# Layer 3 of a four-layer convolution kernel: two samples at a time, transfers over all partitions, a ring of 8 KB chunks

## The chip, the cores and the metric

The kernel runs on one core of a Trainium2 chip. The metric is the device time of one execution in microseconds; lower is better. A core has five engines that take their own instructions in order and meet through semaphores: TensorE (PE, the matmuls), VectorE (DVE), ScalarE (ACT), GpSimd (POOL) and SyncE (SP, which here only issues transfers). The 16 DMA engines move data between the chip's memory (HBM) and the on-chip buffer of 128 partitions (SBUF). Matmuls write to PSUM, and ScalarE or VectorE reads it from there.

## What is computed

The input is `x` with 16 samples, 16 channels and 256 x 256 pixels, in 32-bit floats. Four layers follow each other, each of the form "group norm, a convolution, add to x". The first is a circular 3 x 3 convolution written with Fourier transforms, the second a 5 x 5 convolution of diagonal kernels, the third a spectral layer with poles and residues. Only the fourth, layer 3, is changed:

```python
n = 2.0 ** (ACTBIT - 1) - 1.0                                  # 127
scale_input = jnp.max(jnp.abs(x_cl)) / 2.0 ** (ACTBIT - 1)     # over all samples
x_q = jnp.round(jnp.clip(x_cl / scale_input, -n, n))
acc = lax.conv_general_dilated(x_q, w_hwio, window_strides=(1, 1), padding=((1, 1), (1, 1)), ...)
out = acc * (scale_input * scale_weight) + bias
...
x = x + _L3_conv_ref(_gn(x), ...)
```

So each sample is normalised, divided by one scale that holds for all samples, rounded to whole numbers, clipped to +-127, convolved with a 3 x 3 kernel over 16 channels, scaled, and added to the sample as it came in. Because the scale is a maximum over everything, layer 3 can start on no sample before layer 2 has ended on all; layer 2 writes its result to HBM (`x3d`), and layer 3 reads it back.

## The kernel before

Layers 0 and 1 run together sample by sample, then layer 2 in several stages, then layer 3. Instructions of an engine stand in one fixed order. A scheduler makes that order when the program is built, from the program's text and the dependences between tiles; it puts work of a coming sample among that of the current one. A tile comes from a pool with a number of buffers (`bufs`): one more tile than there are buffers waits until the oldest has been read for the last time, by engines and by transfers.

Layer 3 before, lines 1180 to 1253 (the last `with ExitStack()` of the function `layers`), takes one sample b after the other.

- A sample's 256 rows of 16 channels are laid out as 64 partitions (16 channels times 4 strips s of 64 rows), and a strip is cut into 4 groups g of R = 16 rows. Partitions 0 to 63 (half a = 0) hold groups 0 and 3, partitions 64 to 127 (half a = 1) groups 1 and 2. `of_half` (L1189) gives that view of a tensor in HBM for one half.
- A sample is one tile `xt4` of 32 KB per partition (2 groups x 16 rows x 256 pixels), in a pool of 3. It is loaded in 4 chunks of RC = 4 rows, each by two transfers of 64 partitions, 512 KB each, on the SP queue (L1226).
- For each chunk ScalarE normalises and scales to `u` (L1233, all 128 partitions at once; for the second chunk, the `moved` one, in four pieces of 64 partitions, L1230). VectorE rounds `u` in place by adding and subtracting a large number (L1234) and clips it to `q` in 16-bit floats (L1238 in four pieces, or L1236 at once). A piece moves a group from its partition half a to an operand half h, since the matmul reads 64 partitions of `q` (half h) and writes 64 partitions of PSUM (half a).
- `q` has two buffers, used in turn by even and odd samples, with zero columns at both sides set once, in layer 2's stage (L1132, L1133). GpSimd copies four halo rows to `qh` (L1241).
- The convolution is done in 8 tiles t of 2 rows (`conv`, L1192 to L1218): 9 taps times 4 combinations of (a, h), each a matmul of 64 x 64 weights over 512 columns, four of them side by side in the array. At the edge of a group a matmul is split into two of 256 columns, one reading the neighbouring group or `qh`. Tiles go 1, 2, ... 7, 0, because tile 0 needs the halo above. PSUM holds 4 tiles.
- ScalarE evicts each tile with scale and bias to `o` (L1245), VectorE adds it to the rows of `xt4` in place (L189, the helper `tt` called at L1248), and GpSimd issues the store of a finished chunk to `out`, again two transfers of 64 partitions (L1252). The first chunk goes out last, after tile 0.

What the changed lines depend on: the loads of a sample wait for all stores of the sample three before it, which had the same buffer. In ScalarE's order, the `u` of a coming sample stand among the evictions `o` of an earlier one.

The stage before (layer 2's last, L1002 to L1174) ends with statistics over all samples, the scale by which everything is divided, and the per-sample factors `a3` and `b3` (L1171), one column per sample, the same for both partition halves.

Of the kernel before, what the change touches and what calls it, by code (L numbers as in the profile page):

```python
# [49 lines left out]
F32 = mybir.dt.float32  # L50
BF16 = mybir.dt.bfloat16
AF = mybir.ActivationFunctionType
# [5 lines left out]
P = 128  # L58
C = 16
S = 4  # L60
R = 16
RC = 4
N = 256
# [101 lines left out]
def layers(ctx, tc, x, w0, w1, w3, sw, bias, ty, tx, p1a, p1b, p1c, p2a, p2b, p2c, resa, resb,  # L165
           const, rows, out):
    nc = tc.nc
    B = x.shape[0]
# [4 lines left out]
    dram = ctx.enter_context(tc.tile_pool(name="dram", bufs=1, space=DRAM))  # L173
    x2d = [dram.tile([C, N, N], F32, tag=f"x2d{b}", name=f"x2d{b}") for b in range(B)]
    x3d = [dram.tile([C, N, N], F32, tag=f"x3d{b}", name=f"x3d{b}") for b in range(B)]
# [822 lines left out]
    qs = [last_.tile([P, 2, R, 260], BF16, tag=f"q{k}", name=f"q{k}") for k in range(2)]  # L998


    with ExitStack() as es:
# [97 lines left out]
        with tc.manual_schedule(engines={mybir.EngineType.PE}):  # L1099
            before = None  # L1100
            exps = exponentials(0)
            for k in range(0, C, 2):
                for b in range(B):
# [25 lines left out]
                    if k == C // 2 and b == 0:  # L1129
                        wt = strip_weights(last_, w3, 9, BF16, "wt3", [(0, 0, 9, 0), (9, 0, 3, 1), (12, 6, 3, 2)])  # L1130
                        for q in qs:
                            Q.memset(q[:, :, :, 0:2], 0.0)  # L1132
                            Q.memset(q[:, :, :, 258:260], 0.0)  # L1133
# [46 lines left out]
    with ExitStack() as es:  # L1180
        xp = es.enter_context(tc.tile_pool(name="e_x", bufs=3))
        up = es.enter_context(tc.tile_pool(name="e_u", bufs=3))
        hp = es.enter_context(tc.tile_pool(name="e_h", bufs=2))
        rp = es.enter_context(tc.tile_pool(name="e_r", bufs=4))
        ps_c = es.enter_context(tc.tile_pool(name="e_ps", bufs=4, space=PSUM))
        half = [slice(0, 64), slice(64, P)]
        groups = ((0, 0), (1, 0), (1, 1), (0, 1))

        def of_half(d, a, rr):  # L1189
            g = slice(1, 3) if a else slice(0, 4, 3)  # L1190
            return d.rearrange("c (s g r) w -> (c s) g r w", g=4, r=R)[:, g, rr, :]

        def conv(q, qh, t):

            ps = ps_c.tile([P, 2, 2, N], F32, tag="ps_c", name="ps_c")
            work = [[], [], [], []]
            for dy in (0, -1, 1):
                for dx in (0, -1, 1):
                    near = 3 * (1 + dy) + 1 + dx
                    cols = slice(2 + dx, 2 + dx + N)  # L1200
                    r0 = 2 * t + dy
                    for n, (a, h) in enumerate(groups):
                        o = ps[half[a], h]
                        if 0 <= r0 and r0 + 2 <= R:
                            work[n].append((h, o, near, q[half[h], a, r0 : r0 + 2, cols]))
                            continue
                        for r in range(2):
                            if 0 <= r0 + r < R:
                                work[n].append((h, o[:, r], near, q[half[h], a, r0 + r, cols]))
                            elif n ^ 1 == n + dy:  # L1210
                                work[n].append((h, o[:, r], near, q[half[h], 1 - a, (r0 + r) % R, cols]))
                            else:
                                w = near if 0 <= n + dy < 4 else (9 if dy < 0 else 12) + 1 + dx
                                work[n].append((h, o[:, r], w, qh[half[h], int(dy > 0), cols]))
            for i in range(len(work[0])):
                for h, o, w, src in (work[n][i] for n in (0, 2, 1, 3)):
                    nc.tensor.matmul(o, lhsT=wt[half[h], w, :], rhs=src, start=i == 0, stop=i == len(work[0]) - 1)  # L1217
            return ps  # L1218

        for b in range(B):  # L1220
            xt = xp.tile([P, 2, R, N], F32, tag="xt4", name=f"xt4_{b}")
            q = qs[b % 2]
            for r in range(0, R, RC):
                rr = slice(r, r + RC)
                for a in range(2):
                    nc.sync.dma_start(xt[half[a], :, rr, :], of_half(x3d[b], a, rr))  # L1226
                u = up.tile([P, 2, RC, N], F32, tag="u", name="u")
                moved = r == RC
                for a, h in groups if moved else ():
                    nc.scalar.activation(u[half[h], a], xt[half[a], h, rr, :], AF.Identity,  # L1230
                                         bias=b3[half[a], b : b + 1], scale=a3[half[a], b : b + 1])
                if not moved:
                    nc.scalar.activation(u, xt[:, :, rr, :], AF.Identity, bias=b3[:, b : b + 1], scale=a3[:, b : b + 1])  # L1233
# [5 lines left out]
            qh = hp.tile([P, 2, 260], BF16, tag="qh", name="qh")  # L1239
            for h, k, a, r in ((0, 0, 0, R - 1), (0, 1, 1, 0), (1, 0, 1, R - 1), (1, 1, 0, 0)):  # L1240
                Q.tensor_copy(qh[half[h], k], q[half[1 - h], a, r])  # L1241
            for t in (*range(1, R // 2), 0):
# [3 lines left out]
                xr = xt[:, :, 2 * t : 2 * t + 2, :]  # L1246
                tt(V, xr, xr, o, ADD)
                if t == 0 or t > 1 and t % 2:  # L1248
                    r0 = 2 * t // RC * RC
                    rr = slice(r0, r0 + RC)  # L1250
                    for a in range(2):
                        Q.dma_start(of_half(out[b], a, rr), xt[half[a], :, rr, :])  # L1252
# [89 lines left out]
```

## Time and profile before

| what | value |
|---|---|
| time, median of 3 runs | 4583.26 us (4581.63 to 4588.8) |
| the profiled execution: time, span | 4588.1 us, 4586.3 us |
| layer 3 in it: last statistic read, first load issued, end | 4053.7, 4064.2, 4586.3 us |
| layer 3, from 4080 us: bytes moved, mean rate | 131.8 MB, 258 GB/s |
| layer 3, from 4080 us: share of the 16 DMA engines, loads and stores | 45.8% and 40.2% |
| a load of 512 KB (`xt<-x3d`), median from issue to landing | 12.5 us |
| a store of 512 KB (`out_dram<-xt`), median from issue to landing | 8.3 us |

The engines in 50-us stretches of layer 3 (start:end, length; then busy us and count of TensorE, its weight loads, VectorE, ScalarE, GpSimd; TensorE's granted clock as a share of full, DMA share, GB/s):

```profile
4170.00:4220.00 50.00, 30.70 (x491) 18.47 (x484) 39.47 (x41) 33.58 (x26) 13.26 (x17) 0.84 0.88 258
4270.00:4320.00 50.00, 31.87 (x492) 19.05 (x488) 38.80 (x42) 32.68 (x25) 13.48 (x17) 0.85 0.86 260
4370.00:4420.00 50.00, 32.79 (x568) 20.43 (x564) 39.66 (x43) 31.40 (x24) 14.00 (x18) 0.90 0.84 251
```

How to read the profile: it is one execution, recorded by the hardware. A line of the group table names a source line, an engine, an operation, what it writes and reads (output<-inputs), the shape and the count; then the busy time of all, the mean of one in ns, the idle time of the engine just ahead of them and what ended it. A wait is put down to the event that came last. The DMA share is the part of the 16 engines' time in which a packet was under way, whatever its rate.

### The profile page before, as it was taken

How to read it: one execution, taken by the hardware profiler on the slowest of the kernel's cores; microseconds unless marked ns; L12 is line 12 of the kernel's file. 1: busy time of each engine (PE TensorE's matmuls, PEld its weight loads, DVE VectorE, ACT ScalarE, POOL GpSimd, SP SyncE). 2: the span in 40 equal slices, each digit the busy share in tenths (PEclk: the TensorE clock that was granted, in tenths of full speed). 3: DMA queues.
4: the chain of work that ended last, by engine and by line, in shares of the span. 5: the costliest groups of instructions: out<-in, count | busy, mean ns of one | idle time of the engine just before them, and what ended most of it. 6: DMA issues, size and time to landing. Idle time of an engine off the chain costs nothing. (4 is left out here: it accounts for less than half of the span.)

```text
span 4586.3 us, 123297 instructions
## 1 busy us (share of the span) xinstructions
PE 4004.8 (87%) x50992; PEld 3081.6 (67%) x50992; DVE 3077.3 (67%) x5698; ACT 2708.7 (59%) x3619; POOL 2270.4 (50%) x3562
## 2 busy tenths in 40 slices
PE   5999999999849998999899999997999999955655
PEld 1555555555529998999777777776788888833333
DVE  4767666767578787877655555544666667677767
ACT  3776868686524443444488888885444444446565
POOL 2242323233336555555566666655777777742323
PEclk9999999999979999999999999998999999978888
DMA  6676767685434444445377777777888888769888
GB/s 145 157 186 151 190 147 192 144 197 145 100 100 155 145 156 144 151 146 163 96 159 168 167 171 165 167 166 207 220 220 218 221 225 237 216 193 271 245 261 249
DMA packets 433391, 820.58 MB, mean 179 GB/s; under 512 B 43648, under 2 KB 308864, under 8 KB 417408
## 3 DMA queue, kind: packets, MB, share of 16 engines
q1 hardware_dynamic: 366272, 577.53, 50.2%
q0 software_dynamic: 66560, 235.18, 17.1%
q8 instruction: 402, 6.59, 0.7%
q14 instruction: 157, 1.29, 0.1%
HBM read 408.85 MB, written 336.07 MB: 162 GB/s over the span
## 5 line engine op out<-in xcount | busy, mean ns | idle before, releaser
L381 PE MATMUL ps<-va,wt 128*64 128x512 f32 (+1 forms) x1632 | 668.7, 571 | 11.4 <-POOL va L353 9.3
L381 PE MATMUL ps<-vb,wt 128*64 128x512 f32 (+1 forms) x1632 | 667.1, 570 | 4.7 <-DMA vb<-va 4.7
L877 ACT COPY sk<-ps_s 64x516 f32<-64x516 f32 x1016 | 592.6, 583 | 115.8 <-PE ps_s L872 96.3
L770 ACT ACTIVATE y<-ps_y,bc 128x384 f32<-128x384 f32 x512 | 296.9, 581 | 426.4 <-PE ps_y L768 426.4
L872 PE MATMUL ps_s<-t,l 128*128 128x258 f32 x2048 | 521.4, 397 | 17.8 <-ACT sk L877 8.4
L189 DVE TENSOR_TENSOR ob<-ps_m,other 128x256 f32<-128x256 f32 x512 | 270.9, 607 | 357.3 <-ACT other L965 352.8
L402 ACT ACTIVATE v<-xt,nm 32x2048 f32<-32x2048 f32 x248 | 497.1, 2005 | 9.7 <-PE ps L416 3.5
L416 PE MATMUL ps<-v,w1s 128*64 128x259 f32 x4096 | 481.6, 394 | 11.0 <-DVE v L400 6.7
L1217 PE MATMUL ps_c<-q,wt 64*64 64x512 bf16 (+1 forms) x4800 | 305.6, 403 | 207.1 <-ACT o L1245 179.2
L872 PEld LDWEIGHTS ps_s<-t,l 128*128 128x128 f32 x2048 | 371.1, 191 | 92.2 <-ACT sk L877 8.4
L381 PEld LDWEIGHTS ps<-va,wt 128*64 128x64 f32 x1632 | 223.2, 137 | 305.1 <-issue 271.2
L416 PEld LDWEIGHTS ps<-v,w1s 128*64 128x64 f32 x4096 | 335.2, 141 | 134.7 <-issue 24.0
L1079 PE MATMUL ps_o<-exp,fs 128*128 128x128 f32 x2048 | 404.6, 280 | 19.1 <-ACT fs L1125 19.1
L1217 PEld LDWEIGHTS <-wt 64*64 64x64 bf16 x4992 | 185.7, 115 | 326.8 <-issue 264.2
L1078 PE MATMUL ps_o<-c_last,zt 128*128 128x128 f32 x2048 | 404.1, 280 | 0.2
L1078 PEld LDWEIGHTS ps_o<-c_last,zt 128*128 128x128 f32 x2048 | 329.0, 196 | 63.2 <-issue 62.4
L940 PEld LDWEIGHTS ps_m<-z,sk 128*32 128x32 f32 x16384 | 254.6, 110 | 132.8 <-issue 111.4
L940 PE MATMUL ps_m<-z,sk 128*32 128x64 f32 x16384 | 304.0, 222 | 42.5 <-issue 38.5
L189 POOL TENSOR_TENSOR acc<-acc,prod 128x256 f32<-128x256 f32 x240 | 228.7, 953 | 217.3 <-DVE prod L189 210.8
L189 POOL TENSOR_TENSOR w<-rq 128x512 f32<-128x512 f32 x256 | 320.7, 1280 | 26.4 <-ACT rq L1080 23.6
L1079 PEld LDWEIGHTS ps_o<-exp,fs 128*128 128x128 f32 x2048 | 319.1, 197 | 20.1 <-ACT fs L1125 20.1
L765 PE MATMUL ps_y<-c_y,qd 128*128 128x128 f32 x2048 | 316.8, 278 | 5.3 <-ACT y L770 5.3
(345 smaller groups left out, 8910.0 us busy)
## 6 DMA issues: line engine op xcount, KB each, us to landing
xt<-x2d SPq DMA_DIRECT2D x256, 512.0 KB, 4.4
z<-alphad SPq DMA_DIRECT2D x516, 129.0 KB, 4.9
xt<-in_x_dram SPq DMA_DIRECT2D x256, 256.0 KB, 7.3
x2d<-x2s POOLq DMA_DIRECT2D x256, 256.0 KB, 5.0
mixd<-ob SPq DMA_DIRECT2D x128, 512.0 KB, 5.9
ot<-mixd SPq DMA_DIRECT2D x256, 256.0 KB, 7.3
x3d<-xt POOLq DMA_DIRECT2D x128, 512.0 KB, 5.8
xt<-x3d SPq DMA_DIRECT2D x128, 512.0 KB, 12.5
```

Of the source, the lines that this page charges most:

```text
L189: eng.tensor_tensor(o, a, b, op)
L381: nc.tensor.matmul(ps[halves[h], lo:hi, :], lhsT=wt0[:, w, :], rhs=v[:, 2 * t + lo : 2 * t + hi, j : j + N], start=j == 0 and k == 0, stop ...
L402: nc.scalar.activation(to, o.xt[c][q_], AF.Identity, bias=o.g.nm[q_, 1:2])
L416: nc.tensor.matmul(ps[halves[h], k, 0:U], lhsT=o.w1[:, w : w + 64], rhs=v1[:, lo : lo + U], start=first_, stop=not first_)
L765: nc.tensor.matmul(to[:, :, a, :], lhsT=v[:, c, a, i % 2, :], start=a == 0, stop=a == 1, rhs=y1[:, a].rearrange("p (r f) -> p r f", r=2))
L770: nc.scalar.activation(y[:, c, :], ps[:, 0 : 3 * P], AF.Copy, scale=bc2[:, b, i // 2, 0:1])
L872: nc.tensor.matmul(ps[:, d, 0 : 2 * NX], lhsT=ls[h][:, k + d - k0], rhs=t2[:, h, k + d].rearrange("p x r -> p (x r)"), start=True, stop=True)
L877: copy(sks[2 * e8 + n][64 * h : 64 * h + 64, :, 2 * k : 2 * k + 4] .rearrange("p x (k r) -> p x k r", r=2), ps[64 * n : 64 * n + 64, :, 0 ...
L940: nc.tensor.matmul(to, lhsT=sk[:, x_], rhs=z[:, :, x_], start=True, stop=True)
L1078: nc.tensor.matmul(ps[:, a, c, :], lhsT=zts[d][:, a, c, :], rhs=last[:, c, :], start=True, stop=False)
L1079: nc.tensor.matmul(ps[:, a, c, :], lhsT=fs[:, d, a, :], rhs=ey[:, d, c, :], start=False, stop=True)
L1217: nc.tensor.matmul(o, lhsT=wt[half[h], w, :], rhs=src, start=i == 0, stop=i == len(work[0]) - 1)
```

## The change

Layer 3 takes two samples a = 0, 1 at a time, one in each partition half, and every transfer spans all 128 partitions.

- A group now has R = 32 rows, so a strip has two groups h = 0, 1. A partition half is a sample, an operand half h is a half strip: the matmul for (a, h) reads `q[half h]` with index a and writes PSUM half a.
- `x3d` of two samples is one HBM tensor, and `by_strip` gives a view of 128 partitions (sample, channel, strip). A chunk is 4 rows of both half strips of both samples: one transfer of 1 MB, 8 KB per partition.
- Chunks are tiles of their own: chunk 0 of each pair from the pool `e_f` with 2 buffers (it is stored last), chunks 1 to 7 from `e_x` with 10. A chunk is stored as soon as both of its tiles are added, chunk 0 after tile 0.
- Chunks 1, 3, 5, 7 are `moved` (four ScalarE pieces, one clip on VectorE), the others the reverse.
- The pair is convolved in 16 tiles, 1 to 15 and then 0. Rows beyond a half strip come from `qh`, now with both samples in one copy (four copies of 64 x 2 x 260).
- `u` has 2 buffers for 3, `o` 3 for 4. `q` is twice as large, belongs to this stage's pools, and its zero columns are set at the start of it. `a3` and `b3` are copied to `a3p` and `b3p` with a column per pair (four small copies).

The built order on the engines follows the scheduler as before; on SP the 64 loads of 1 MB stand in the order of their chunks, with chunk 0 of a pair behind its chunks 1 to 3 from the third pair on. On GpSimd the stores stand in the order of the tiles, with the halo copies of the next pair among them: two behind the store of chunk 1, two ahead of that of chunk 7.

```diff
--- before.py
+++ after.py
@@ -58,7 +58,7 @@
 P = 128
 C = 16
 S = 4
-R = 16
+R = 32
 RC = 4
 N = 256
 NX = 129
@@ -172,7 +172,8 @@
 
     dram = ctx.enter_context(tc.tile_pool(name="dram", bufs=1, space=DRAM))
     x2d = [dram.tile([C, N, N], F32, tag=f"x2d{b}", name=f"x2d{b}") for b in range(B)]
-    x3d = [dram.tile([C, N, N], F32, tag=f"x3d{b}", name=f"x3d{b}") for b in range(B)]
+    x3p = [dram.tile([2, C, N, N], F32, tag=f"x3d{k}", name=f"x3d{k}") for k in range(B // 2)]
+    x3d = [x3p[b // 2][b % 2] for b in range(B)]
     alphad = dram.tile([N, 2, 2, 8, B // BG, NX, BG], F32, tag="alphad", name="alphad")
     mixd = dram.tile([N // 2, 4, C, 2, 2, B, 32], F32, tag="mixd", name="mixd")
 
@@ -995,7 +996,6 @@
     mn3 = last_.tile([P, G2], F32, tag="mn3", name="mn3")
     a3 = last_.tile([P, B], F32, tag="a3", name="a3")
     b3 = last_.tile([P, B], F32, tag="b3", name="b3")
-    qs = [last_.tile([P, 2, R, 260], BF16, tag=f"q{k}", name=f"q{k}") for k in range(2)]
 
 
     with ExitStack() as es:
@@ -1128,9 +1128,6 @@
                     before = (b, k, zts, fs, exps[1], xt)
                     if k == C // 2 and b == 0:
                         wt = strip_weights(last_, w3, 9, BF16, "wt3", [(0, 0, 9, 0), (9, 0, 3, 1), (12, 6, 3, 2)])
-                        for q in qs:
-                            Q.memset(q[:, :, :, 0:2], 0.0)
-                            Q.memset(q[:, :, :, 258:260], 0.0)
                 exps = coming
             along_x(*before)
 
@@ -1178,22 +1175,28 @@
 
 
     with ExitStack() as es:
-        xp = es.enter_context(tc.tile_pool(name="e_x", bufs=3))
-        up = es.enter_context(tc.tile_pool(name="e_u", bufs=3))
+        xp = es.enter_context(tc.tile_pool(name="e_x", bufs=10))
+        fp = es.enter_context(tc.tile_pool(name="e_f", bufs=2))
+        up = es.enter_context(tc.tile_pool(name="e_u", bufs=2))
         hp = es.enter_context(tc.tile_pool(name="e_h", bufs=2))
-        rp = es.enter_context(tc.tile_pool(name="e_r", bufs=4))
+        rp = es.enter_context(tc.tile_pool(name="e_r", bufs=3))
         ps_c = es.enter_context(tc.tile_pool(name="e_ps", bufs=4, space=PSUM))
+        qp = es.enter_context(tc.tile_pool(name="e_q", bufs=1))
+        qs = [qp.tile([P, 2, R, 260], BF16, tag=f"q{k}", name=f"q{k}") for k in range(2)]
+        for q in qs:
+            Q.memset(q[:, :, :, 0:2], 0.0)
+            Q.memset(q[:, :, :, 258:260], 0.0)
         half = [slice(0, 64), slice(64, P)]
-        groups = ((0, 0), (1, 0), (1, 1), (0, 1))
-
-        def of_half(d, a, rr):
-            g = slice(1, 3) if a else slice(0, 4, 3)
-            return d.rearrange("c (s g r) w -> (c s) g r w", g=4, r=R)[:, g, rr, :]
+        groups = [(a, h) for h in range(2) for a in range(2)]
+        chunks = R // RC
+
+        def by_strip(d):
+            return d.rearrange("b c (s h r) w -> (b c s) h r w", s=S, h=2)
 
         def conv(q, qh, t):
 
             ps = ps_c.tile([P, 2, 2, N], F32, tag="ps_c", name="ps_c")
-            work = [[], [], [], []]
+            work = [[] for _ in groups]
             for dy in (0, -1, 1):
                 for dx in (0, -1, 1):
                     near = 3 * (1 + dy) + 1 + dx
@@ -1207,49 +1210,53 @@
                         for r in range(2):
                             if 0 <= r0 + r < R:
                                 work[n].append((h, o[:, r], near, q[half[h], a, r0 + r, cols]))
-                            elif n ^ 1 == n + dy:
-                                work[n].append((h, o[:, r], near, q[half[h], 1 - a, (r0 + r) % R, cols]))
                             else:
-                                w = near if 0 <= n + dy < 4 else (9 if dy < 0 else 12) + 1 + dx
-                                work[n].append((h, o[:, r], w, qh[half[h], int(dy > 0), cols]))
+                                w = near if h == (dy < 0) else (9 if dy < 0 else 12) + 1 + dx
+                                work[n].append((h, o[:, r], w, qh[half[h], a, int(dy > 0), cols]))
             for i in range(len(work[0])):
                 for h, o, w, src in (work[n][i] for n in (0, 2, 1, 3)):
                     nc.tensor.matmul(o, lhsT=wt[half[h], w, :], rhs=src, start=i == 0, stop=i == len(work[0]) - 1)
             return ps
 
-        for b in range(B):
-            xt = xp.tile([P, 2, R, N], F32, tag="xt4", name=f"xt4_{b}")
-            q = qs[b % 2]
-            for r in range(0, R, RC):
-                rr = slice(r, r + RC)
-                for a in range(2):
-                    nc.sync.dma_start(xt[half[a], :, rr, :], of_half(x3d[b], a, rr))
+        a3p, b3p = (hp.tile([P, B // 2], F32, tag=k, name=k, bufs=1) for k in ("a3p", "b3p"))
+        for a in range(2):
+            for to, src in ((a3p, a3), (b3p, b3)):
+                V.tensor_copy(to[half[a]], src[half[a]].rearrange("p (k a) -> p k a", a=2)[:, :, a])
+        for k in range(B // 2):
+            q = qs[k % 2]
+            xs = []
+            for j in range(chunks):
+                rr = slice(RC * j, RC * j + RC)
+                pool = xp if j else fp
+                xt = pool.tile([P, 2, RC, N], F32, tag="xt4", name=f"xt4_{k}_{j}")
+                xs.append(xt)
+                nc.sync.dma_start(xt, by_strip(x3p[k])[:, :, rr, :])
                 u = up.tile([P, 2, RC, N], F32, tag="u", name="u")
-                moved = r == RC
+
+                moved = j % 2
                 for a, h in groups if moved else ():
-                    nc.scalar.activation(u[half[h], a], xt[half[a], h, rr, :], AF.Identity,
-                                         bias=b3[half[a], b : b + 1], scale=a3[half[a], b : b + 1])
+                    nc.scalar.activation(u[half[h], a], xt[half[a], h], AF.Identity,
+                                         bias=b3p[half[a], k : k + 1], scale=a3p[half[a], k : k + 1])
                 if not moved:
-                    nc.scalar.activation(u, xt[:, :, rr, :], AF.Identity, bias=b3[:, b : b + 1], scale=a3[:, b : b + 1])
+                    nc.scalar.activation(u, xt, AF.Identity, bias=b3p[:, k : k + 1], scale=a3p[:, k : k + 1])
                 V.tensor_scalar(u, u, ROUND, ROUND, ADD, SUB)
                 if moved:
                     V.tensor_scalar(q[:, :, rr, 2 : 2 + N], u, 127.0, -127.0, ALU.min, ALU.max)
                 for a, h in () if moved else groups:
                     V.tensor_scalar(q[half[h], a, rr, 2 : 2 + N], u[half[a], h], 127.0, -127.0, ALU.min, ALU.max)
-            qh = hp.tile([P, 2, 260], BF16, tag="qh", name="qh")
-            for h, k, a, r in ((0, 0, 0, R - 1), (0, 1, 1, 0), (1, 0, 1, R - 1), (1, 1, 0, 0)):
-                Q.tensor_copy(qh[half[h], k], q[half[1 - h], a, r])
+            qh = hp.tile([P, 2, 2, 260], BF16, tag="qh", name="qh")
+            for n, r in ((1, 0), (0, R - 1)):
+                for h in range(2):
+                    Q.tensor_copy(qh[half[h], :, n], q[half[1 - h], :, r])
             for t in (*range(1, R // 2), 0):
                 ps = conv(q, qh, t)
                 o = rp.tile([P, 2, 2, N], F32, tag="o", name="o")
                 nc.scalar.activation(o, ps, AF.Identity, bias=bi, scale=so)
-                xr = xt[:, :, 2 * t : 2 * t + 2, :]
+                j, r = divmod(2 * t, RC)
+                xr = xs[j][:, :, r : r + 2, :]
                 tt(V, xr, xr, o, ADD)
-                if t == 0 or t > 1 and t % 2:
-                    r0 = 2 * t // RC * RC
-                    rr = slice(r0, r0 + RC)
-                    for a in range(2):
-                        Q.dma_start(of_half(out[b], a, rr), xt[half[a], :, rr, :])
+                if t == 0 or j and r == RC - 2:
+                    Q.dma_start(by_strip(out[2 * k : 2 * k + 2])[:, :, RC * j : RC * j + RC, :], xs[j])
 
 
 def laid_out(inputs):
```

## The prediction

> **What bounds the kernel now.** Only layer 3, the last 530 us, is changed, so I read that stretch alone: who waits, then one turn of its loop in time order, then the rate of the transfers, then what each instruction costs. The waits from 4080 us to the end (who waited for whom, us in total, times, longest), the DMA-issuing queue's own in the second fence:
>
> ```profile
> PE ps_c L1217 <- ACT o L1245: 179.2, 56, 12.1
> ACT u L1233 <- DMA xt<-x3d: 161.2, 31, 12.8
> ```
>
> ```profile
> SPq L1226 <- DMA out_dram<-xt: 337.7, 52, 21.6
> ```
>
> Read from the bottom: the loads wait for stores, ScalarE waits for loads, TensorE waits for ScalarE to empty PSUM. ScalarE takes its instructions in order, and a normalisation of a coming sample (`u`) stands in front of evictions (`o`) of the current one. One such stop, in the timeline of ScalarE (start, length; idle before in brackets):
>
> ```profile
> 4282.13 2.29 ACT L1245 ACTIVATE o<-ps_c,bi,so 128x1024 f32<-128x1024 f32 x2
> 4295.87 2.09 ACT L1233 ACTIVATE u<-xt,b,a 128x2048 f32<-128x2048 f32 x1 [11.44 <-DMA xt<-x3d]
> 4297.87 1.19 ACT L1245 ACTIVATE o<-ps_c,bi,so 128x1024 f32<-128x1024 f32 x1
> ```
>
> The next stop ends at 4328.90, so a sample takes 33.0 us and a pair 66.0. The period is a closed loop: the last eviction of a sample started at 4274.86, its addition ended at 4279.19, its last store landed at 4287.79, the load into that buffer was issued at 4287.93, its second half landed at 4295.76, `u` started at 4295.87. In the next turn this loop latency is 20.0 us (4308.87 to 4328.90), and ScalarE needs 13.0 us from that `u` to the next last eviction: 20.0 + 13.0 = 33.0. So the stage is bound neither by an engine nor by bytes, but by buffer reuse: store, landing, load, landing.
>
> The rates, from the windows (length, ScalarE busy and count, granted clock, DMA share, GB/s):
>
> ```profile
> 4068.00:4092.00 24.00, 14.68 (x10) 0.68 1.03 221
> 4292.00:4298.00 6.00, 2.13 (x2) 0.75 1.02 222
> 4336.00:4342.00 6.00, 5.96 (x5) 1.00 1.02 399
> 4564.00:4582.00 18.00, 4.69 (x4) 0.80 0.99 369
> ```
>
> All DMA engines are busy in each row, yet they move 221 where loads of 64 partitions run alone and about 400 where loads and stores, or stores of both halves, overlap. The busy share hides a factor of two.
>
> The costs, from 4080 us on (busy us, mean ns | idle before):
>
> ```profile
> L189 DVE TENSOR_TENSOR xt<-xt,o 128x1024 f32<-128x1024 f32 x128 | 158.4, 1250 | 31.9 <-ACT o L1245 30.5
> L1245 ACT ACTIVATE o<-ps_c,bi,so 128x1024 f32<-128x1024 f32 x128 | 148.9, 1196 | 10.7 <-DVE xt L189 5.3 <-PE ps_c L1217 4.4
> L1233 ACT ACTIVATE u<-xt,b,a 128x2048 f32<-128x2048 f32 x47 | 98.3, 2092 | 164.9 <-DMA xt<-x3d 161.2 <-DVE q L1238 1.9 <-DVE q L1236 1.5
> L1230 ACT ACTIVATE u<-xt,b,a 64x1024 f32<-64x1024 f32 x60 | 74.1, 1235 | 1.4 <-DMA xt<-x3d 0.5
> ```
>
> Last, one transfer of 512 KB with nothing beside it, a load (4064.20) and a store (4342.23), from issue to landing:
>
> ```profile
> DMA to landing us min/median/max: 5.2/5.2/5.2
> ```
>
> ```profile
> DMA to landing us min/median/max: 4.6/4.6/4.6
> ```
>
> **What the Trainium skill says.** SBUF — State Buffer, section "Door 1: The DMA port swizzle": partitions 0 to 63 reach only 8 of the 16 ports, about 218 GB/s, and all 128 reach 16. The 221 and the 400 above agree. DMA: Bandwidth & Descriptors, section "Rules for kernel authors": use one transfer of 128 partitions instead of two of halves. Same page, section "Anatomy of one DMA": some 2 us of a transfer do not depend on its bytes. Here 512 KB at 221 GB/s is 2.4 us, which leaves 2.8 of the load's 5.2 and 2.2 of the store's 4.6: fixed cost, a little above that.
>
> **The change part by part.** *Transfers.* 1 MB over 128 partitions at 410 GB/s takes 2.6 us. Not seen before in this shape: estimate 2.8 + 2.6 = 5.4 us for a load, 2.2 + 2.6 = 4.8 for a store. The bounds: 4.6 and 4.4 if the fixed part is the skill's 2 us, 7.6 and 7.0 if the full width moves only 221. Three full-width loads of 512 KB at 1294 us landed 1.5 and 1.4 us apart, which speaks for the fast end.
>
> *Engine work per pair.* Of its 8 chunks 4 are normalised in four half-width pieces (2 of 8 before). ScalarE: 4 x 2.09 + 16 x 1.235 + 16 x 1.196 = 47.3 us (41.7 for two samples before). VectorE: 8 roundings x 1.24, 4 clips x 1.24, 16 half clips x 0.709, 16 additions x 1.25 = 46.2 (49.4 before). TensorE: 192 matmuls fewer, 16 tiles of 2.15 us at full clock = 34. None reaches 66, so these edits cost nothing by themselves while reuse sets the pace. GpSimd copies twice as many halo elements per copy (1.13 us before): 1 to 2 us, counted in the chain below.
>
> *The ring.* Chunks 1 to 7 of a pair take 10 buffers in turn, chunk 0 takes 2 of its own. So chunk 4+i of a pair reuses the buffer of chunk 1+i of the pair before it, chunks 1 to 3 that of 5 to 7 two pairs back, and chunk 0 that of chunk 0 two pairs back. ScalarE's built order in a steady turn, with t for an eviction of pair k and u for a normalisation of pair k+1 (four pieces in odd chunks): t1 t2 u0 t3 u1 t4 u1 u2 t5 u3 t6 u3 u4 t7 t8 u5 t9 u5 t10 u6 t11 u7 t12 u7 t13 t14 t15 t0. Chunk j is stored after tile 2j+1, chunk 0 after t0, which is the last tile. Each store-to-load path gives a wait if its latency exceeds ScalarE's work between its two ends:
>
> - H: t0 of a pair to u0 two pairs later stands only t0, t1, t2 apart: 3.6 us.
> - B: t5 to u5: four evictions, u3, u4: 11.8 us.
> - D: t9 to u7: three evictions, one piece of u5, u6: 6.9 us.
> - The others (t3 to u4 16.8, t11 to u1 17.8, t13 to u2 16.6, t15 to u3 18.7) are longer than the latency below; t7 to u6 (9.7) overlaps B and D and gives less.
>
> H, B and D do not overlap, so the turn is 47.3 - 3.6 - 11.8 - 6.9 = 25.0 us plus the three latencies. One latency, alone: eviction 1.27, addition 1.23, to the store's issue 0.3, store 4.8, to the load's issue 0.14, load 5.4, start 0.08: 13.2 us. B adds 0.2 for the rounding ahead of its addition on VectorE: 13.4. D: 13.2. H is worse: VectorE stands behind u7's rounding and clip and four additions (7.5 us from u7's end, 3.6 us ahead of t0), so the store is issued at 4.3 and not 2.8; GpSimd has the store of chunk 7 right before it, and loads of chunks 2 and 3 share the engines (2.6 us each): store landed near 11.7, load near 17.2. Sum 43.8, turn 68.8 us against 66.0. What is queued behind each stopped `u` is the evictions, and TensorE behind them with at most 4 tiles ahead. The gain in rate is thus spent: before, there was one reuse loop in 33 us, now three in 69.
>
> *Start and end.* Both first chunk-0 buffers lie where the last buffers of the stage before are free near 4055 us, so `u0` has its data when the scales are ready (4065 us, four tiny copies included). Chunk 1 is issued at 4064.2 as before, landed at 4069.6. From there no reuse wait binds in the first turn: u1 to u7 26.0, pair 1's u 28.1, 15 evictions 17.9, so t0 of pair 0 starts at 4141.7. Moving `q` out of the older pool shifts layer 2's tiles and puts three small loads on the SP queue ahead of that stage's first data: 3 x 0.55 = 1.6 us (0 to 3). So 4143. Then 6 turns: 413, to 4556. The last pair has no normalisations: 15 tiles x 2.0 us (spacing of evictions at the end of before) plus 4 for the clock, which falls to 0.5 in stops, then 2.8 to the store, 5.5 landing, 2.5 to the end: 44. Sum 4600 us against the profiled span of 4586.3: +13.5. The profiled execution took 4588.1 with what lies around its span; the median of the runs is 4583.3. I set the difference on the median: 4597.
>
> **Rivals.**
> - The latencies come out shorter: fixed parts of 2 us, no queueing in H: 12, 12 and 14.5. Turn 63.5, six turns save 32 us: 4565, faster. It decides in ScalarE's stops at u0, u5, u7: below 41.5 us in sum the turn falls under 66.5, the break-even. For it: 400 GB/s is seen. Against it: VectorE's backlog at t0 and three stores in 5 us.
> - The ring's waits are covered and ScalarE and VectorE set the pace, some 50 us a turn: 4597 - 6 x 18.8 = 4484. Against it: H's 3.6 us of cover for two transfers.
> - The full width is no faster than half, 7.6 and 7.0 per transfer: latencies near 17.6, 17.6, 23, turn 83, 4597 + 86 = 4683. Against it: the windows near 400.
>
> **How the numbers follow.** Forecast 0.68 (4575 to 4625: +-3 us on the sum of latencies, +-8 on the ends), short latencies 0.20, engine pace 0.06, half rate 0.06. Range 4563 to 4640, leaving out the last two. A difference under 0.2% (9 us) can't be told from none. Slower: 0.50 of the forecast and the half rate, 0.56. Same: 0.15 of the forecast. Faster: the rest, 0.29.
>
> **What would show it.** Right: ScalarE idle before `u` in three places of each turn, over 10 us at chunk 0, 1 to 7 at chunks 5 and 7; loads waiting for `out_dram` in the DMA queue's waits; 1 MB landing in about 5 us; a turn of 66 to 72 us. Wrong: no idle at chunk 0, or rates near 220 GB/s with all engines busy, or VectorE busy over 85% of the stage.

## The result and the profile after

| what | before | after |
|---|---|---|
| time, median of 4 runs each | 4584.4 us (4581.63 to 4588.8) | 4642.53 us (4635.04 to 4647.67) |
| ratio of after to before, 95% interval | | 1.0125 (1.0107 to 1.0142) |
| span of the profiled execution | 4586.3 us | 4645.9 us |
| a pair of samples in a steady turn | 66.0 us | 75.6 us |

The changed kernel is 58 us slower. Layer 3's waits after the change, from 4080 us on (who waited for whom: us in total, times, longest), first for the engines:

```profile
PE ps_c L1218 <- ACT o L1254: 222.3, 57, 16.9
ACT u L1241 <- DMA xt<-x3d: 123.3, 12, 19.3
...
ACT u L1238 <- DMA xt<-x3d: 45.2, 13, 6.1
```

then for the queue that issues the loads:

```profile
SPq L1233 <- DMA out_dram<-xt: 475.5, 52, 30.7
```

It is the same chain as before: loads wait for stores (475.5 us, was 337.7), ScalarE waits for loads (123.3 + 45.2 = 168.5, was 161.2), TensorE waits for ScalarE (222.3, was 179.2). ScalarE's waits for loads grew by only 7 us, however. From the first `u` to the end, layer 3 takes 514.0 us before and 571.8 after; ScalarE (length; busy us and count; clock, DMA share, GB/s), before and after:

```profile
4072.30:4586.30 514.00, 321.54 (x240) 0.85 0.87 260
4074.10:4645.90 571.80, 370.70 (x288) 0.78 0.64 232
```

Of the 58 us more, 49 are ScalarE at work (four of the eight chunks of two samples are now normalised in four pieces, two before) and 9 are idle. How much fewer pieces would give back was not tried. It need not be all of it, as work that stands between a store and the `u` that waits for it only shortens the stop there.

The three places of a turn at which ScalarE stops are in its timeline (start, length; idle before in brackets), at `u` of chunks 0, 5 and 7:

```profile
4225.41 4.49 ACT L1254 ACTIVATE o<-ps_c,bi,so 128x1024 f32<-128x1024 f32 x4
4230.77 1.21 ACT L1254 ACTIVATE o<-ps_c,bi,so 128x1024 f32<-128x1024 f32 x1 [0.86 <-PE ps_c L1218]
4232.96 1.21 ACT L1254 ACTIVATE o<-ps_c,bi,so 128x1024 f32<-128x1024 f32 x1 [0.99 <-PE ps_c L1218]
4251.29 2.09 ACT L1241 ACTIVATE u<-xt,b3p,a3p 128x2048 f32<-128x2048 f32 x1 [17.12 <-DMA xt<-x3d]
...
4262.63 1.19 ACT L1254 ACTIVATE o<-ps_c,bi,so 128x1024 f32<-128x1024 f32 x1
...
4276.20 3.74 ACT L1238 ACTIVATE u<-xt,b3p,a3p 64x1024 f32<-64x1024 f32 x3 [1.95 <-DMA xt<-x3d]
4279.96 1.20 ACT L1254 ACTIVATE o<-ps_c,bi,so 128x1024 f32<-128x1024 f32 x1
...
4294.41 1.24 ACT L1238 ACTIVATE u<-xt,b3p,a3p 64x1024 f32<-64x1024 f32 x1 [6.03 <-DMA xt<-x3d]
```

The lone `o` at 4262.63 is t5, the one at 4279.96 is t9. So chain B took 4276.20 - 4262.63 = 13.57 us and D 4294.41 - 4279.96 = 14.45 us. For H, t0 of the pair before, the last of the four evictions in the first line, started at 4228.69, and u0 at 4251.29: 22.6 us. The prediction's sum, 25.0 us plus the three latencies, gives 25.0 + 22.60 + 13.57 + 14.45 = 75.6 us for this turn, which took 75.1. Over the six steady turns (first evictions of the pairs, 4154.4 to 4607.8) the mean turn is 75.6 us, with mean latencies of 22.9, 13.4 and 14.7; that leaves 24.5 us where the forecast had 25.0.

The transfers did become faster. The loads' row (issues, KB each, median us from issue to landing), to be read against 12.5 us for 512 KB before:

```profile
xt<-x3d SPq DMA_DIRECT2D x55, 1024.0 KB, 5.6
```

They are also used less. The windows (length; busy us and count of TensorE, weight loads, VectorE, ScalarE, GpSimd; clock, DMA share, GB/s) show DMA shares of 0.54 to 0.70 where they were 0.84 to 0.88, and no engine near its limit:

```profile
4170.00:4220.00 50.00, 26.40 (x336) 14.85 (x336) 34.34 (x35) 34.01 (x26) 6.05 (x7) 0.73 0.54 194
4270.00:4320.00 50.00, 32.66 (x484) 19.47 (x477) 30.10 (x28) 27.74 (x22) 7.69 (x8) 0.84 0.70 249
4370.00:4420.00 50.00, 25.37 (x380) 15.79 (x383) 26.42 (x25) 29.74 (x25) 8.79 (x9) 0.75 0.62 220
```

### The profile page after: what moved, and what is told of

Its sections match the earlier page's. It is cut to its first block, busy times and chain, and to the rows that moved or that the text cites. A ratio compares the mean times of both kernels' runs of the same rounds, so it can differ in the third digit from the quotient of the medians.

```text
span 4645.9 us, 122584 instructions
## 1 busy us (share of the span) xinstructions
PE 4031.7 (87%) x50800; PEld 3086.6 (66%) x50800; DVE 3061.4 (66%) x5654; ACT 2759.6 (59%) x3667; POOL 2204.4 (47%) x3466
## 5 line engine op out<-in xcount | busy, mean ns | idle before, releaser
L1218 PE MATMUL ps_c<-q,wt 64*64 64x512 bf16 (+1 forms) x4608 | 330.4, 441 | 238.7 <-ACT o L1254 222.3
L1218 PEld LDWEIGHTS <-wt 64*64 64x64 bf16 x4800 | 198.1, 124 | 371.6 <-issue 313.7
L1079 PEld LDWEIGHTS ps_o<-exp,fs 128*128 128x128 f32 x2048 | 316.7, 195 | 17.4 <-ACT fs L1125 17.4
```

Of the source, the lines that this page charges most:

```text
L1079: nc.tensor.matmul(ps[:, a, c, :], lhsT=fs[:, d, a, :], rhs=ey[:, d, c, :], start=False, stop=True)
```

## The experiments

Two questions were asked of the chip. Why does chain H take 22.6 us instead of the 17.2 forecast? And what sets the turn at all: the ring and the order of the tiles, the transfers, or the places that the scheduler gives to `u`? All times are medians; the ratio to the kernel before, run beside each, follows with its 95% interval. The kernels were timed at different times, beside a kernel before of 4579.8 to 4584.4 us: a difference between two of them in us comes out up to 7 us other if it is taken from the ratios.

### Chunk 0 stored early

```diff
-            for t in (*range(1, R // 2), 0):
+            for t in (1, 2, 3, 0, *range(4, R // 2)) if k else (*range(1, R // 2), 0):
```

> From the second pair on, tile 0 is computed after tile 3 and chunk 0 is stored there; else the changed kernel. Theory (a turn is 25.0 us plus the latencies of the three reuse chains; measured 22.6 for chunk 0, 13.6 for chunk 5, 14.5 for chunk 7): the stop before u of chunk 0 vanishes, as its buffer comes back twelve tiles earlier, so a turn is 25.0 + 3.6 + 13.6 + 14.5 = 56.7 us instead of 75.6. The first pair keeps its order, so one long stop stays; five turns save 19 us each: about 4642 - 95 = 4547 us. Rival 1 (the transfers' total rate sets the pace, the stops only show where it is felt): the idle time moves to chunks 5 and 7, the turn stays above 70 us, 4620 to 4645 us. Rival 2 (the delay sits in VectorE's and GpSimd's backlog, wherever the store stands): a new stop of some 10 us elsewhere, 4590 to 4610 us.

Measured: 4667.07 us (1.0188, 1.0171 to 1.0205), slower than the changed kernel by 25 us, and outside all three expectations. A steady turn is now some 81 us. ScalarE's timeline:

```profile
4258.89 2.09 ACT L1241 ACTIVATE u<-xt,b3p,a3p 128x2048 f32<-128x2048 f32 x1 [6.90 <-DMA xt<-x3d]
4260.89 4.47 ACT L1254 ACTIVATE o<-ps_c,bi,so 128x1024 f32<-128x1024 f32 x4
4278.12 3.74 ACT L1238 ACTIVATE u<-xt,b3p,a3p 64x1024 f32<-64x1024 f32 x3 [12.76 <-DMA xt<-x3d]
```

Between t5, the first of the four evictions at 4260.89, and u5 at 4278.12 stands 4.5 us of work. In the changed kernel 11.8 us stood there. The edit did not touch these two, but the scheduler had made a new order. ScalarE's instructions of a turn as built (t evictions, u normalisations, ' of the pair after the next):

```
changed kernel  t1 t2 u0 t3 u1 u1 t4 u1 u1 u2 t5 u3 u3 u3 t6 u3 u4 t7 t8 u5 u5 u5 t9 u5 t10 u6 ...
                ... t11 u7 t12 u7 u7 u7 t13 t14 t15 t0
tile 0 early    u2 t1 t2 u3 t3 u3 u3 u3 t0 t4 u4 t5 t6 t7 t8 u5 u5 u5 t9 u5 u6 t10 t11 u7 t12 ...
                ... u7 u7 u7 t13 u0' u1' t14 u1' u1' u1' t15
```

With chunk 0 free earlier, the scheduler moved u0 and u1 into the turn before and u3 and u4 ahead of t5, so that only evictions are left between t5 and u5. From t5 to u5 passed 17.2 us, more than the 13.6 of the changed kernel, so the latency did not stay the same either. The idle time went to other chunks, as rival 1 said; whether for its reason, the transfers' rate, was left to the runs by hand below. My theory took the order of the other instructions and the other latencies as fixed; that is what fell.

### One ring of 12

```diff
-                pool = xp if j else fp
-                xt = pool.tile([P, 2, RC, N], F32, tag="xt4", name=f"xt4_{k}_{j}")
+                xt = xp.tile([P, 2, RC, N], F32, tag="xt4", name=f"xt4_{k}_{j}")
...
-            for t in (*range(1, R // 2), 0):
+            for t in (1, 2, 3, 0, *range(4, R // 2)) if k else (*range(1, R // 2), 0):
```

(`xp` has 12 buffers, `fp` is gone.)

> As the run with tile 0 early, and all eight chunks of a pair take their buffers from one ring of 12 (the same bytes of SBUF), so that each chunk reuses the buffer of the chunk four further on two pairs back, or of the chunk four back one pair back. Theory: every store then has 14 us or more of ScalarE's work before the load that waits for it is needed, and a latency alone is 13.2 to 14.5 us: no stop above 1 us is left, the turn is ScalarE's and VectorE's own work, 47.3 us, to 50 us; one first stop stays; 4490 to 4510 us, under both kernels. Rival (transfers or VectorE set the pace before that): the turn stays at 56 us or more, as with tile 0 early alone, 4545 us or more.

Measured: 4669.40 us (1.0193, 1.0176 to 1.0209). A miss of the same kind: a ring in which every buffer has more time to come back gives the same slow turn, about 81 us, in yet another order of `u`. ScalarE's waits for loads:

```profile
ACT u L1236 <- DMA xt<-x3d: 155.5, 24, 8.6
...
ACT u L1239 <- DMA xt<-x3d: 48.7, 20, 6.6
```

204 us in 44 stops, none over 8.6 us: more and shorter than the 168.5 in 25 of the changed kernel.

### Chunk 0 loaded first

```diff
+        es.enter_context(tc.manual_schedule(engines={mybir.EngineType.SP}))
```

Under `manual_schedule` an engine keeps the order of the program's text. Here it holds for the loads of layer 3; in the traces the orders of ScalarE, VectorE and GpSimd are those of the changed kernel.

> The changed kernel with the loads of layer 3 issued in the order 0, 1, 2, ... 7 of each pair, where the scheduler had put chunk 0 behind chunks 1, 2 and 3. Chunks 1 to 3 are then not loaded while the store of chunk 0 is under way. Theory (the chain of chunk 0 takes 22.6 us, not the 17.2 forecast, since its store waits for a load's whole transfer of 1 MB): its store lands 7 to 8 us after its issue instead of 12.4, the stop before u of chunk 0 shrinks by some 5 us, the turn is 70 to 72 us, with 1 or 2 us given back at chunks 1 to 3: 4615 to 4625 us. Rival (the store of chunk 7 ahead of it and VectorE's backlog make the delay): the store still takes 12 us, and chunks 1 to 3, now late, add stops of their own: 4642 to 4670 us.

Measured: 4608.57 us (1.0063, 1.0042 to 1.0084), 34 us faster than the changed kernel and a little under the 4615 to 4625 us expected; a turn is 70.0 us. The store of chunk 0, issued 4.9 us after t0 in both kernels, took from issue to landing, first in the changed kernel:

```profile
DMA to landing us min/median/max: 12.4/12.4/12.4
```

and with chunk 0's load first:

```profile
DMA to landing us min/median/max: 7.0/7.0/7.0
```

The difference of 5.4 us is about twice the 2.6 us that a transfer of 1 MB holds the engines (the prediction's estimate). In the changed kernel two loads are under way beside this store: that of chunk 2, issued 0.7 us ahead of it, and that of chunk 3, issued 5.2 us after it and landed 1.6 us after it. What each of the two costs was not separated. The store of chunk 7 is ahead of it in both kernels. One chain H of this run: t0, the last of the four evictions in the first line, at 4284.75, and u0 at 4302.04:

```profile
4281.47 4.49 ACT L1255 ACTIVATE o<-ps_c,bi,so 128x1024 f32<-128x1024 f32 x4
4287.85 1.21 ACT L1255 ACTIVATE o<-ps_c,bi,so 128x1024 f32<-128x1024 f32 x1 [0.35 <-DVE xt L190]
4302.04 2.09 ACT L1242 ACTIVATE u<-xt,b3p,a3p 128x2048 f32<-128x2048 f32 x1 [12.98 <-DMA xt<-x3d]
```

That is 17.3 us (17.4 on the mean of six turns), the forecast's figure of 17.2. But the forecast was for the kernel with the two loads, which it named, and here they are out of the way.

### Half-width transfers

```diff
-                nc.sync.dma_start(xt, by_strip(x3p[k])[:, :, rr, :])
+                for a in range(2):
+                    nc.sync.dma_start(xt[half[a]], by_strip(x3p[k])[half[a], :, rr, :])
...
-                    Q.dma_start(by_strip(out[2 * k : 2 * k + 2])[:, :, RC * j : RC * j + RC, :], xs[j])
+                    for a in range(2):
+                        Q.dma_start(by_strip(out[2 * k : 2 * k + 2])[half[a], :, RC * j : RC * j + RC, :], xs[j][half[a]])
```

> The changed kernel with each load and each store of 1 MB split into two of 64 partitions, 512 KB each, issued one after the other on the same queue: same bytes, same order, same ring. Theory (width sets a lone transfer's speed): each half moves at 220 GB/s if the two halves are served one after the other, so a load takes 7.6 and a store 7.0 us, each chain 4.4 us longer and chunk 0's more, as it stands behind two others; a turn 75.6 + 13 to 18 us, six turns: 4720 to 4750 us. If the two halves, issued 0.6 us apart, move side by side, only the second issue is paid, 1.2 us a chain: 4660 to 4670 us. Rival (the turn isn't set by the transfers' duration): no change, 4642 us.

Measured: 4623.83 us (1.0093, 1.0074 to 1.0111), 19 us faster than the changed kernel, where 18 to 108 us slower was expected. Here, too, the scheduler had put ScalarE's work in another order (u0 after four tiles instead of two, for one), so the run tells nothing of the width. It was repeated with ScalarE's order and that of the loads written out as the changed kernel has them (VectorE's and GpSimd's stayed with the scheduler, and VectorE's differs in a few places of a turn):

> The changed kernel with each load and store split into two of 64 partitions, as in the run with half-width transfers, but with ScalarE's order and the order of the loads held at those of the changed kernel; in that run the scheduler had moved u of chunk 0 two tiles later. Theory (width counts): the second half of a load lands some 1.8 us and that of a store 2.5 us later than the whole, by the lone ones of that run, so each chain is 4 us longer, the turn 85 to 93 us, six turns: 4700 to 4750 us. Rival (full width earns nothing): 4642 us.

Measured: 4702.53 us (1.0271, 1.0257 to 1.0285), 60 us slower than the changed kernel; a turn is 84.5 us. ScalarE's waits for loads:

```profile
ACT u L1249 <- DMA xt<-x3d: 169.6, 21, 23.6
...
ACT u L1246 <- DMA xt<-x3d: 57.6, 22, 6.0
```

227 us against 168.5: 59 us, about the whole difference. In one chain B the two halves of the load were issued at 4286.34 and 4286.90 and landed at 4291.37 and 4293.69: 7.35 us from the first issue to the last landing, against 5.6 for one whole load. So the full width is worth about 9 us a turn in this order, as far as VectorE's small changes don't add to it.

### The order of four engines written by hand

The bodies of the loop became functions `normalise(k, j)` and `tile_of(k, t)`, called in the order in which they are to run. That sets the order of ScalarE, VectorE, GpSimd and the loads at once; the loads keep the order that they have in a steady turn of the changed kernel. Ring, tiles and transfers are those of the changed kernel:

```diff
+        es.enter_context(tc.manual_schedule(engines={mybir.EngineType.SP, mybir.EngineType.Activation, mybir.EngineType.DVE, mybir.EngineType.Pool}))
...
+        slot = {2: (1,), 4: (2,), 6: (3,), 7: (0,), 9: (4,), 11: (5,), 13: (6,), 15: (7,)}
+        for j in range(chunks):
+            normalise(0, j)
+        halo(0)
+        for k in range(B // 2):
+            for n, t in enumerate((*range(1, R // 2), 0)):
+                tile_of(k, t)
+                for j in slot.get(n + 1, ()) if k + 1 < B // 2 else ():
+                    normalise(k + 1, j)
+            if k + 1 < B // 2:
+                halo(k + 1)
```

> The changed kernel, same ring (10 and 2 buffers), tiles and transfers, with layer 3's order written by hand for ScalarE, VectorE, GpSimd and the loads: the u of the coming pair stand evenly among the evictions, in the order of chunks 1, 2, 3, 0, 4, 5, 6, 7, after 2, 4, 6, 7, 9, 11, 13 and 15 tiles. Every store then has six or seven tiles, 17 us or more of ScalarE's work, before the u that reuses its buffer. Theory (the turn is 25 us plus three latencies because the scheduler puts each u where it takes the data to be there, too early): no stop above 2 us in a steady turn, which is then ScalarE's own 47.3 us, to 52: six turns save 23 to 28 us each, 4475 to 4505 us, under both kernels. Rival (with the stops gone the transfers, 16.8 MB a pair in and 16.8 out, set the pace): 33.6 MB at 400 GB/s are 84 us, so the turn stays at 75 us or more and the time within 20 us of 4642.

(The rival's figure there counts the bytes twice: a turn moves 16.8 MB in all, 8.4 in and 8.4 out, 42 us at 400 GB/s. So its 75 us was no bound.)

Measured: 4494.21 us (0.9811, 0.9798 to 0.9825), 148 us faster than the changed kernel and 1.9% faster than the one before. ScalarE's waits for loads and TensorE's for ScalarE:

```profile
PE ps_c L1218 <- ACT o L1260: 111.0, 37, 12.6
...
ACT u L1239 <- DMA xt<-x3d: 21.5, 14, 2.9
ACT u L1242 <- DMA xt<-x3d: 15.2, 12, 4.3
```

36.7 us instead of 168.5. The transfers' rate, 230 GB/s on the mean in the changed kernel, was thus not what held its turn at 75.6. A turn is 51.6 us on the mean of six, against 75.6: six times 24 us are 144. Two windows of it, in which ScalarE is busy for 45 of 50 us and the DMA share is over 0.9 at 329 and 344 GB/s:

```profile
4150.00:4200.00 50.00, 35.91 (x592) 22.69 (x588) 43.55 (x44) 44.98 (x37) 9.37 (x11) 0.90 0.92 329
...
4250.00:4300.00 50.00, 35.67 (x599) 22.39 (x595) 42.78 (x44) 45.02 (x36) 10.27 (x12) 0.93 0.98 344
```

The same was done to the ring of 12:

> The run with one ring of 12 buffers and tile 0 after tile 3, which took 4669 us, with the order written by hand: one u after every second tile, chunks 0 to 7 in turn. The only difference to that run is the order of the instructions. Theory (the scheduler's places for u, not the ring, set the turn): no stop above 2 us, 47.3 to 52 us a turn, 4475 to 4505 us. Rival (transfer rate): a turn of 75 us or more, 4640 us or more. If the scheduler's order were as good as any, 4669 us.

Measured: 4497.22 us (0.9821, 0.9806 to 0.9836), 172 us under the same ring in the scheduler's order, and like the ring of 10 and 2. So the order decides, and between these two rings there is no difference. What each of the four engines' orders contributes was not separated; that ScalarE's waits for loads fell by 132 us points to the places of `u`.

With the good order, the width was tried again (each load and store of the run at 4494 us split into halves):

> The changed kernel in the order written by hand (4494 us), with each load and store split into two of 64 partitions. Theory (width matters for the rate as well as for a lone transfer): the DMA engines are 92% busy there at 325 GB/s, so transfers that hold an engine twice as long while alone lengthen the turn from 52 to 55 to 62 us: 4515 to 4565 us. Rival (with six tiles of cover the width no longer shows, since halves of different transfers overlap): within 10 us of 4494.

Measured: 4535.08 us (0.9893, 0.9876 to 0.9909), 41 us more; a turn is 56 us, and the DMA share is 1.0 at 300 GB/s:

```profile
4250.00:4300.00 50.00, 31.93 (x495) 19.40 (x488) 36.51 (x36) 41.60 (x33) 12.07 (x18) 0.86 1.02 300
```

### The kernel before, in an order written by hand

Tiles, pool of 3 and half-width transfers of the kernel before; only the loop is written as above, with a `normalise` after every second tile.

```diff
+        for b in range(B):
+            for n, t in enumerate((*range(1, R // 2), 0)):
+                tile_of(b, t)
+                if n % 2 and b + 1 < B:
+                    normalise(b + 1, n // 2 * RC)
+            if b + 1 < B:
+                halo(b + 1)
```

> The kernel before, its tiles, pool of 3 and half-width transfers unchanged, with layer 3's order written by hand as in the run that took 4494 us: one u of the next sample after every second tile. A sample's buffer then comes back with a whole sample's tiles (25 us) and two more between its last store and the u that needs it, against a latency of 20 us. Theory (the scheduler's order cost the kernel before its 33 us a sample, too, and the change of layout is not needed): VectorE's 24.7 us a sample set the pace, 25 to 27 us a sample, 4480 to 4515 us, within 0.5% of the changed kernel in the same order. Rival (half-width transfers cap the rate): at the 258 GB/s of the stage before, 8.4 MB in and out take 32.5 us a sample, and the time stays near 4580; with a rate between these, 4520 to 4560 us, and the new layout is worth the difference to 4494.

Measured: 4479.41 us (0.9771, 0.9751 to 0.9790), the fastest of all, 2.3% under the kernel before and some 15 us under the changed kernel in its good order. Two samples take 48.9 us on the mean, against 66.0. Two windows:

```profile
4200.00:4250.00 50.00, 37.84 (x625) 22.39 (x624) 48.87 (x52) 41.47 (x33) 25.08 (x24) 0.97 1.02 346
4250.00:4300.00 50.00, 38.01 (x634) 23.28 (x637) 48.82 (x53) 40.27 (x31) 25.08 (x24) 0.97 1.01 343
```

VectorE is busy for 98% of them, and so are the DMA engines. The new layout isn't needed for the gain, and in a good order it shows none of its own. Nearly all of the 15 us lies at the start: from its first load to its first eviction layer 3 takes 24.8 us here (4056.9 to 4081.7) and 42.3 (4053.4 to 4095.7) in the run at 4494, which normalises a whole pair first. From the first eviction to the end the two take 395.9 and 397.0 us: the turn is shorter here (48.9 against 51.6), the end longer.

### The move of `q` alone

The kernel before, with `q` and its zero columns in layer 3's own pool:

```diff
-    qs = [last_.tile([P, 2, R, 260], BF16, tag=f"q{k}", name=f"q{k}") for k in range(2)]
...
+        qp = es.enter_context(tc.tile_pool(name="e_q", bufs=1))
+        qs = [qp.tile([P, 2, R, 260], BF16, tag=f"q{k}", name=f"q{k}") for k in range(2)]
```

> The kernel before with one edit of the change alone: the two tiles q and their zero columns are moved from the pool of the stage before to layer 3's own. Forecast by the prediction: 1.6 us later (0 to 3). Theory now (the last statistic came 8.8 us later in the changed kernel, of which 3 us were there before layer 2's last stage): 5 to 6 us, a ratio of 1.0012. Rival (the shift was one execution's): 0 to 1 us.

Measured: 4583.85 us, a ratio of 1.0006 (0.9999 to 1.0013), so +2.7 us with an interval from about 0 to 6. It doesn't tell the forecast's 1.6 us from 5; the theory that all of the 8.8 us came from the change is out. The traces say the same: the six other kernels that have `q` moved and the ring of 10 and 2 issue their first load at 4050.9 to 4055.3 us, the changed kernel's own trace at 4063.9. Most of its late start belongs to that one execution.

## Why the prediction was right or wrong

- **The mechanism was right.** Reuse of buffers sets the turn, ScalarE stops at chunks 0, 5 and 7 (17 to 19, 2, and 5 to 6 us), loads wait for `out_dram`, 1 MB lands in 5.6 us, and the sum "25.0 us plus the three latencies" holds to 0.5 us a turn. Slower was the likelier side.
- **Chain H was mis-sized, and it is the step that failed.** The prediction says "loads of chunks 2 and 3 share the engines (2.6 us each): store landed near 11.7". It landed 17.2 us after t0, and H took 22.9 us instead of 17.2 (means of six turns). The figure of 11.7 is 4.3 to the issue, 4.8 for a lone store, and 2.6 for one transfer beside it. The issue came at 4.9, and the store then took 12.4 us instead of 7.4, as three transfers were ahead of it or beside it: the store of chunk 7, which the sentence names, and both loads. With the loads out of the way the same store landed 11.8 us after t0 and H took 17.4 us, as the chapter on chunk 0 loaded first shows. Six turns times 5.7 us are 34 of the 45 us by which the forecast fell short.
- **Chain D** took 14.7 us on the mean, not 13.2: its store took 6.1 us in the turn shown (4.9 to 7.0 in the six), beside the load of chunk 6, and not the 4.8 of a lone one. Six turns: 9 us. **Chain B** was right (13.4 on the mean), and the rest of the turn was 0.5 us too long (25.0 against 24.5).
- **That "these edits cost nothing by themselves while reuse sets the pace"**, as the prediction says of the engines' work, doesn't fit its own sum, in which ScalarE's work on a pair stands with 47.3 us, 5.6 more than before. The forecast has it in its number, but not in its account of the loss: ScalarE was busy for 49 us more in layer 3.
- **The price of width** was right in kind. The rival with half rates is out: with ScalarE's order held, halves cost 60 us more, and 41 with all four engines' orders held. The estimates of a lone load and store, 5.4 and 4.8 us, were met (5.3 to 5.6 and 4.4 to 4.7), not the 7.6 and 7.0 of half the rate. This agrees with the Trainium skill, SBUF — State Buffer, section "Door 1: The DMA port swizzle", on which they rest. The section "Anatomy of one DMA", from which the prediction has its 2 us, is about transfers issued by GpSimd, so about the stores; for the loads only the traces speak. And whole transfers gave the changed kernel no lead over the kernel before with its halves, once both had a good order (4494 against 4479 us).
- **Start and end.** In the trace the last `t0` of the first pair was 10 us later than forecast, 8.8 of it ahead of layer 3, and the end took 5 us less than 44. The experiment on `q` leaves 0 to 6 us of the start to the change, with 1.6 forecast.
- **"The engine pace, some 50 us a turn"**, given 0.06, did not come with this change. It was in reach, though, by the order alone: 51.6 us a turn in the run by hand. The prediction read ScalarE's order from the build and took its places as a fact of the ring ("t0, t1, t2 apart: 3.6 us"). They are a choice of the scheduler, which in every version left to it put some `u` too close behind the store it waits for. Why it takes data to be there so early was not tried; its planning isn't visible in a trace.

What the summed terms explain: turns 6 x 6.8 = 41 us, start +10, end -5, which is 46 us from the forecast span of 4600 to the measured 4645.9. In the medians it is 58.1 against 13.5, so 45.

## What to carry to other kernels

Where engines run in one fixed order and a scheduler makes it, the distance between a store and the work that needs its buffer again is set by that order as much as by the number of buffers. Here two rings took the same time (4667 and 4669 us in the scheduler's orders, 4494 and 4497 in those by hand), and the order by hand took 148 us off the changed kernel. So look at the built order first, and spread the waiting instructions by hand before a layout is changed. An experiment that changes a ring, a tile order or a transfer must hold the order of the other instructions, or it measures a new order. When a reuse chain is summed, count the transfers that are under way ahead of the store and beside it, loads of the other queue as well: here two loads added 5.4 us to one store.

## What the runs showed of the hardware

- A store of 1 MB issued 0.7 us after a load of 1 MB on another queue did not share the engines evenly with it: in the changed kernel nearly all packets of the load of chunk 2, issued at 4232.88, started between 4236.4 and 4240.6 us, and those of the store of chunk 0, issued at 4233.55, from 4239.3 on, most of them after 4240.2. The two were served nearly whole, one after the other.
- Half-width transfers reached 343 to 346 GB/s over 50 us at a DMA share of 1.0, in the kernel before with its order by hand, but 300 at the same share in the changed kernel with halves. What makes the difference was not tried.
